# Two context pairs of the first batch: halves split in natural layout and turned by DMA transposes

## The chip, the core and the metric

The kernel runs on one core of one Trainium2 chip. The metric is the time of one execution of the program on the device, in microseconds (us): the median of several executions. The core has five engines, each with its own in-order stream of instructions: PE (TensorE: matmuls, and transposes as matmuls with an identity), DVE (VectorE), ACT (ScalarE), POOL (GpSimd) and SP (SyncE, which here issues every DMA). PEld is PE's loading of weights, which the profile shows apart.

## What is computed

A decoder layer with three sublayers, each followed by a residual sum and a layer norm, on x of 4 x 256 x 512 and a context of 4 x 1601 x 512, in fp32:

```python
x = _layernorm(x + attn(x, ...))           # attention over 16 features of a token, cheap
x = _layernorm(x + xattn(x, ctx, ...))     # nearly all of the work
x = _layernorm(x + ffn(x, ...))            # 64 experts' biases, top 8, cheap

# xattn: 32 query heads, 8 key/value heads of 128
kv = concatenate([context, latents], axis=1)          # 1857 tokens of each batch
q, k, v = latents @ Wq, kv @ Wk, kv @ Wv              # then by heads
q, k = rms_norm(q, q_norm_w), rms_norm(k, k_norm_w)
probs = softmax(q k^T / sqrt(128))
out = (probs v) @ Wo
```

## The kernel before

**Halves.** PE multiplies in fp16. To keep fp32's precision each operand is held as a high half (the value rounded to fp16) and a low half (what the rounding left), and each product is three matmuls: high by high, high by low, low by high (`mm3`, L237 to L243). A `split` (L88) makes the halves: ACT writes the high one (L90), then DVE, or POOL where it is told so, subtracts (L92; L94 where a scale is applied).

**Tiles and units.** The 1857 tokens of a batch are 15 tiles of up to 128 tokens, taken in eight pairs: pairs 0 to 5 are context, pair 6 is the two tiles of the latents (the 256 tokens of x after the first sublayer), pair 7 is the last, short tile of the context. A unit is one key/value head of one batch: 8 heads x 4 batches = 32 units, four query heads each. Per unit, each pair is projected (`kv_proj`, L390: the tile kvp in PSUM), its keys are normalized and split (`kv_n`, L416: the tile kh) and turned by a DMA transpose into KT (`kv_tr`, L431). Per query head come the scores s (`qk`), their copy S and maximum M, the exponentials P with their halves (L545 to L555) and the products o with the values (L574 to L576).

**Turning the input.** PE needs a pair's tokens with the features on the partitions. `kv_make` (L334) does that once per batch and pair, and leaves the halves in kvm, which is stored to DRAM (kvd, `kv_keep`, L364) and loaded again for later units. It has two ways. For the first batch: load the fp32 rows (cst, `src_load`), turn each of the two tiles with four PE transposes into the PSUM tile kvtp (L348), and split from there, ACT and DVE, 128x512 each. For the other batches: split the rows as they are, 128x1024 at once, into the tile nat (which has a single buffer), and turn both halves of both tiles with one DMA transpose (L359). The first batch's pairs stay in SBUF for the first two units, which are projected together. kvm has three buffers, the PSUM tiles six in turn, and kh shares a pool of five buffers with others.

**Order.** The order of the start-up is written out by hand in the string `START` (L29): its words name steps such as load4, make4 (kv_make of pair 4), proj4 (kv_proj for both first units), norm4, turn4, keep4. Between them stand the first sublayer (a0, a1: its results y are the latents), the weights' splits, the q projections. Everything after it is sorted by positions (`at`, L714) from the tables of numbers AT, F0 and LAST. A scheduler then orders the instructions of each engine by its own estimate of their times, so a change in one place can shift neighbours on every engine. An instruction waits at the head of its engine's stream until what it needs is there, and what stands behind it waits too.

Names that the steps use: st_q, st_kv and st_o are loaded weights of Wq, Wk/Wv and Wo before their splits into wq, wkv and wo; kss and krk are the sum of squares and the scale of k (POOL, L405 and L406); bnrs is the scale of a layer norm (POOL, L164); qn, qh and QT are q normalized, split and turned.

Of the kernel before, what the change touches and what calls it, by code (L numbers as in the profile page):

```python
# [19 lines left out]
XS = 1.0  # L20
# [22 lines left out]
          lexp=0.335, lexps=0.178, lpv=2.055, levac=1.151, lout=3.348, lqk=1.003, lqkw=0.833)  # L43

LAST = dict(maxb=0.352, exp=0.478, exps=0.207, evac=1.181, wout=3.893, qk=-2.845, qmax=1.507, norm=1.251, turn=2.762, wo=2.134, bkv=9.818, bq=5.434, bo=2.349, lq1=2.628, srcl=0.453, mke=-2.061, mktl=-1.69, s3i=-0.687, s3w=4.208)
F0 = dict(xm=1, maxt=0.133, maxb=0.145, exp=0.367, exps=0.122, pv=2.25, evac=0.972, out=3.422, wout=4.882, qk=-1.157,
          qmax=0.828, norm=0.349, turn=1.009, lead=3.36, wkv=8.299, wq=6.751, wqs=0.602, wq1=5.352, wo0=2.125,
          wo=0.038, lq1=2.522, l1lo=0.774, l1w=-1.506, srcl=0.65, mklo=0.296, mke=-2.739, mktl=-2.607, prep3=3.901,
          s3=5.222, s3i=0.334, s3w=5.192)
# [2 lines left out]
def tile_decoder(ctx: ExitStack, tc: tile.TileContext, x, cx, Wq1, bq1, Wk1, bk1, Wv1, bv1,  # L52
# [15 lines left out]
    TL = NF // 2  # L68
# [16 lines left out]
    def tps(name):  # L85
        return psu.tile([P, 512], F32, tag="u", name=name)

    def split(dst_h, dst_l, src, scale, eng=None):  # L88

        nc.scalar.activation(dst_h, src, AF.Copy, scale=scale)  # L90
        if scale == 1.0:
            (eng or nc.vector).tensor_tensor(dst_l, src, dst_h, ALU.subtract)  # L92
        else:
            nc.vector.scalar_tensor_tensor(dst_l, src, scale, dst_h, ALU.mult, ALU.subtract)  # L94
# [25 lines left out]
    def eng(k):  # L120
        return nc.gpsimd if k else nc.vector
# [186 lines left out]
    def nk(t):  # L308
        return REM if t == NT - 1 else P

    def kview(tile_, t):

        o = (t % 2) * 2 * NC * P
        return tile_[:, o:o + 2 * NC * P].rearrange("p (l c k) -> p l c k", l=2, c=NC)[:, :, :, :nk(t)]

    def tiles_of(p):
        return [t for t in (2 * p, 2 * p + 1) if t < NT]
# [16 lines left out]
    def kv_make(b, p):  # L334

        kt = pkv.tile([P, 2 * RW], F16, tag="kv", name=f"kvm_{b}_{p}")
        assert p != TL or {("x1", b, 0), ("x1", b, 1)} <= done
        if b == 0:
            for u in range(HB):
                kvt[u, p] = kt  # L340
            if p == NPAIR - 1:
                nc.gpsimd.memset(kt[:, :RW].rearrange("p (a k) -> p a k", k=P)[:, :, REM:], 0.0)
            for t in tiles_of(p):
                k = nk(t)
                tp = tps(f"kvtp_{b}_{t}")
                for c in range(NC):
                    sc = y[b, t - NF][:, c * P:(c + 1) * P] if p == TL else src[b, p][:k, t % 2, c * P:(c + 1) * P]
                    nc.tensor.transpose(tp[:, c * k:(c + 1) * k], sc, ident[:k, :k])  # L348
                v = kview(kt, t)
                split(v[:, 0], v[:, 1], tp[:, :NC * k].rearrange("p (c k) -> p c k", c=NC), XS)  # L350
        else:
            nat = p1.tile([P, 2, 2, E], F16, tag="nat", name=f"nat_{b}_{p}")
            n, k = len(tiles_of(p)), nk(2 * p)
            if k < P:
                nc.gpsimd.memset(nat[64:, 0], 0.0)
            for e, j in enumerate(range(n) if p == TL else (slice(0, n),)):
                sc = y[b, j] if p == TL else src[b, p][:k, j]
                split(nat[:k, j, 0], nat[:k, j, 1], sc, XS, eng(p == TL))
            nc.sync.dma_start(out=kt[:, :n * RW].rearrange("p (a k) -> p a k", k=P),  # L359
                              in_=nat[:, :n].rearrange("p j l e -> p (j l e)"), transpose=True)  # L360
        if b > 0:
            kv_keep(b, p, kt)

    def kv_keep(b, p, kt):  # L364
        nc.sync.dma_start(out=kvd[b][p][:, :width(p)], in_=kt[:, :width(p)])
        done.add(("kvd", b, p))
# [334 lines left out]
    for p in range(NPAIR):  # L701
        for k, f in (("load", src_load), ("make", kv_make), ("keep", lambda b, p: kv_keep(b, p, kvt[b, p]))):
            first[f"{k}{p}"] = lambda f=f, p=p: f(0, p)
        for k, f in (("proj", kv_proj), ("norm", kv_n), ("turn", kv_tr)):
            first[f"{k}{p}"] = lambda f=f, p=p: [f(u, p) for u in range(HB)]
# [15 lines left out]
    def par(u):  # L721
        return dict(AT, **F0) if u < KVH else dict(AT, **LAST) if u >= U - 4 else AT

# [6 lines left out]
    for b in range(1, B):  # L730
        A = par(KVH * (b - 1))
        t0 = 4 * (KVH * b - 1)
        lo = max(t0 + A["l1b"], A["l1lo"])
        for i in range(NQ):
            w = (t0 + A["l1w"] - lo) / NQ
            spread(lo + w * i, lo + w * (i + 1), stage1(b, i), 10)
        new = [p for p in range(NPAIR) if p != TL]
        lo = max(t0 + A["mkb"], A["mklo"])
        for k, p in enumerate(new):
            pos = lo + (t0 + A["mke"] - lo) * k / len(new)  # L740
            at(pos - A["srcl"], src_load, b, p)
            at(pos, kv_make, b, p)
        at(t0 + A["mktl"], kv_make, b, TL)
    for u in range(1, U):
        h, b = units[u]
# [14 lines left out]
    for u in range(U):  # L760
        h, b = units[u]
# [81 lines left out]
```

## Time and profile before

| | |
|---|---|
| runs of the kernel before | 2420.73 us median of 3 (2419.91 to 2424.31) |
| profiled execution | 2421.83 us, its span 2420.10 us |
| busy share of the span | PE 97%, PEld 83%, DVE 79%, ACT 85%, POOL 64% |
| granted TensorE clock, mean | 0.991 |
| DMA | 338.82 MB, 140 GB/s on average |
| `kv_make`, first batch | PE transposes L348 of cst x52; DVE splits of kvtp 128x512 x14, 677 ns each; ACT 604 ns each |
| `kv_make`, other batches | ACT splits of cst 128x1024, 1057 ns (median); DMA transposes L359 x24 |
| POOL subtraction L555, 128x1024 | 2148 ns each, x384 |

The span runs from the first to the last instruction; the time of an execution has a little around it. The profile gives each engine's busy time, and for each idle stretch of an engine the instruction or transfer that ended it ("<-"). The chain of waits follows the end back through what released what. Times in the lines are us from the start of the span: first the start, then the length. Ends of pipelined matmuls are modelled, so the pace of matmuls is read from their starts.

### The profile page before, as it was taken

Reading aid. Unit: us, or ns where it says so; the run is one execution under the profiler, and the core shown is the slowest. Engines: PE = TensorE matmul, PEld = TensorE weight load, DVE = VectorE, ACT = ScalarE, POOL = GpSimd, SP = SyncE. Lnnn points to the kernel's source line nnn. Section 1 sums busy time; section 2 is a strip of 40 time slices with the busy share of each in tenths; the row PEclk is TensorE's granted clock in tenths of the full one; section 3 lists DMA queues with packets and bytes.
Section 4 is the critical chain, followed back from the end, with each engine's and each line's share of the span. In section 5 each row is a group of like instructions: output and inputs, shape, how many; then the busy total and the mean of one; then the engine's idle time right before and its main releaser. Section 6 shows DMA issues by size and latency. Waiting matters only on the chain.

```text
span 2420.1 us, 65667 instructions
## 1 busy us (share of the span) xinstructions
PE 2347.3 (97%) x25424; PEld 2003.1 (83%) x25424; DVE 1909.9 (79%) x3747; ACT 2051.1 (85%) x4672; POOL 1538.5 (64%) x1367
## 2 busy tenths in 40 slices
PE   7799999999999999999999999999999999999997
PEld 5587888888888878888888888888888888888885
DVE  8788978987877788787777788787777778777775
ACT  4798898888888878889888888888889888889884
POOL 2377776776666655776656666666666655657554
PEclk9999999999999999999999999999999999999997
DMA  8946776666564546555545555455644543554310
GB/s 267 245 100 160 185 175 178 185 153 156 137 164 112 148 139 166 139 142 125 151 128 129 156 142 137 140 138 121 156 116 113 131 122 109 140 131 105 98 35 27
DMA packets 393345, 338.82 MB, mean 140 GB/s; under 512 B 318532, under 2 KB 328260, under 8 KB 384840
## 3 DMA queue, kind: packets, MB, share of 16 engines
q1 hardware_dynamic: 393032, 334.63, 53.0%
q8 instruction: 199, 3.26, 0.6%
q14 instruction: 114, 0.93, 0.2%
HBM read 219.98 MB, written 38.80 MB: 107 GB/s over the span
## 4 chain that ended last, share of the span: by engine, by line
PE 74%; ACT 8%; DVE 7%; issue 5%; POOL 4%; DMA 2%; SPq 0%; POOLq 0%; DVEq 0%; ACTq 0%
PE o L574 7%; PE o L576 7%; PE o L575 7%; PE kvp L241 7%; PE kvp L243 7%; PE s L241 7%; PE kvp L242 7%; PE s L243 7%; PE s L242 7%; PE wo L241 2%; PE wo L242 2%; PE wo L243 2%; POOL P L555 2%; DVE S L545 2%; ACT P L553 2%
## 5 line engine op out<-in xcount | busy, mean ns | idle before, releaser
L555 POOL TENSOR_TENSOR P<-S,P 128x1024 f16<-128x1024 f32 (+1 forms) x512 | 1032.3, 2027 | 435.3 <-ACT S L554 410.3
L574 PE MATMUL o<-Vh,P 128*128 128x129 f16 (+1 forms) x3840 | 696.1, 221 | 6.8 <-ACT P L553 2.9
L576 PE MATMUL o<-Vh,P 128*128 128x129 f16 (+1 forms) x3840 | 695.8, 220 | 3.6 <-POOL P L555 3.6
L575 PE MATMUL o<-Vl,P 128*128 128x128 f16 (+1 forms) x3840 | 695.0, 219 | 0.0
L498 ACT COPY S<-s 128x512 f32<-128x512 f32 (+1 forms) x1024 | 568.3, 594 | 81.8 <-PE s L243 75.4
L553 ACT ACTIVATE P<-S,lnps 128x1024 f16<-128x1024 f32 (+1 forms) x480 | 530.9, 1117 | 48.1 <-DVE S L545 46.8
L545 DVE TENSOR_TENSOR S<-S,mt 128x1024 f32<-128x1024 f32 (+1 forms) x512 | 557.8, 1146 | 13.1 <-PE mt L536 12.2
L554 ACT ACTIVATE S<-S,lnps 128x1024 f32<-128x1024 f32 (+1 forms) x480 | 538.4, 1126 | 0.2
L241 PE MATMUL s<-QT,KT 128*128 128x256 f16 x1920 | 524.0, 273 | 14.1 <-ACT S L498 3.1
L243 PE MATMUL s<-QT,KT 128*128 128x256 f16 x1920 | 523.9, 273 | 0.0
L242 PE MATMUL s<-QT,KT 128*128 128x256 f16 x1920 | 523.7, 273 | 0.0
L504 DVE TENSOR_TENSOR M<-s,M 128x512 f32<-128x512 f32 x640 | 438.5, 685 | 99.8 <-ACT S L498 79.6
L574 PEld LDWEIGHTS <-P 128*128 128x128 f16 (+1 forms) x3840 | 376.1, 98 | 24.6 <-DVE oh L593 3.3
L241 PE MATMUL kvp<-wkv_back,kv 128*128 128x256 f16 (+1 forms) x1440 | 392.6, 273 | 1.8 <-DVE rl L584 0.6
L243 PE MATMUL kvp<-wkv_back,kv 128*128 128x256 f16 (+1 forms) x1440 | 392.6, 273 | 0.0
L242 PE MATMUL kvp<-wkv_back,kv 128*128 128x256 f16 (+1 forms) x1440 | 392.6, 273 | 0.0
L575 PEld LDWEIGHTS <-P 128*128 128x128 f16 (+1 forms) x3840 | 377.4, 98 | 14.7
L576 PEld LDWEIGHTS <-P 128*128 128x128 f16 (+1 forms) x3840 | 375.6, 98 | 5.0 <-POOL P L555 3.8
L241 PEld LDWEIGHTS <-kv 128*128 128x128 f16 (+1 forms) x2040 | 201.5, 99 | 48.0 <-issue 8.0
L243 PEld LDWEIGHTS <-kv 128*128 128x128 f16 (+1 forms) x2040 | 201.4, 99 | 47.1
L242 PEld LDWEIGHTS <-kv 128*128 128x128 f16 (+1 forms) x2040 | 201.4, 99 | 41.4 <-issue 1.7
L241 PEld LDWEIGHTS <-KT 128*128 128x128 f16 x1920 | 188.0, 98 | 33.1 <-issue 5.5
(177 smaller groups left out, 4164.2 us busy)
## 6 DMA issues: line engine op xcount, KB each, us to landing
kv<-kvd SPq DMA_DIRECT2D x210, 512.0 KB, 3.7
wq_back<-wqd SPq DMA_DIRECT2D x24, 1024.0 KB, 6.2
wo_back<-wod SPq DMA_DIRECT2D x24, 1024.0 KB, 5.2
kvd<-kvm SPq DMA_DIRECT2D x28, 512.0 KB, 3.1
cst<-in_ctx_dram SPq DMA_DIRECT2D x24, 512.0 KB, 5.8
wkv_back<-wkvd SPq DMA_DIRECT2D x24, 512.0 KB, 4.2
st_q<-in_L_xattn_Wq_dram SPq DMA_DIRECT2D x17, 512.0 KB, 4.8
wqd<-wq SPq DMA_DIRECT2D x8, 1024.0 KB, 6.1
```

The costliest lines, as they stand in the source:

```text
L241: nc.tensor.matmul(dst, ah, bh, start=start and k == 0, stop=False, skip_group_check=skip)
L242: nc.tensor.matmul(dst, ah, bl, start=False, stop=False, skip_group_check=skip)
L243: nc.tensor.matmul(dst, al, bh, start=False, stop=stop and k == n - 1, skip_group_check=skip)
L498: nc.scalar.copy(sv, ps[:, :m, :])
L504: nc.vector.tensor_tensor(Mx[n], ps, Mx[n], ALU.max)
L545: nc.vector.tensor_tensor(sv, sv, Mb[n].unsqueeze(1).broadcast_to([P, m, S]), ALU.subtract)
L553: nc.scalar.activation(pt[:, 0, :m, :], sv, AF.Exp, bias=lnps, scale=ES)
L554: nc.scalar.activation(sv, sv, AF.Exp, bias=lnps, scale=ES)
L555: nc.gpsimd.tensor_tensor(pt[:, 1, :m, :], sv, pt[:, 0, :m, :], ALU.subtract)
L574: nc.tensor.matmul(a[:, :P + 1], ph, v1[:k], start=t == 0 and i == 0, stop=False, skip_group_check=True)
L575: nc.tensor.matmul(a[:, :P], ph, v0[:k], start=False, stop=False, skip_group_check=True)
L576: nc.tensor.matmul(a[:, :P + 1], pl, v1[:k], start=False, stop=t == NT - 1 and i == NQ - 1, skip_group_check=True)
```

## The change

For the first batch, pairs 4 and 5 take the way of the other batches: split as rows into nat and turned by one DMA transpose each. A bit mask, dm=48 (bits 4 and 5), picks them. In this way the first batch has its low halves subtracted on POOL; the other batches keep DVE, except for the latents' pair, which had POOL and keeps it. The store to kvd stays a step of its own for the first batch (keep4, keep5).

```diff
-F0 = dict(xm=1, maxt=0.133, ...
+F0 = dict(dm=48, xm=1, maxt=0.133, ...
...
         if b == 0:
             for u in range(HB):
                 kvt[u, p] = kt
+        turned = b > 0 or F0["dm"] >> p & 1
+        if not turned:
             if p == NPAIR - 1:
                 nc.gpsimd.memset(kt[:, :RW].rearrange("p (a k) -> p a k", k=P)[:, :, REM:], 0.0)
             for t in tiles_of(p):
...
         else:
             nat = p1.tile([P, 2, 2, E], F16, tag="nat", name=f"nat_{b}_{p}")
...
             for e, j in enumerate(range(n) if p == TL else (slice(0, n),)):
                 sc = y[b, j] if p == TL else src[b, p][:k, j]
-                split(nat[:k, j, 0], nat[:k, j, 1], sc, XS, eng(p == TL))
+                split(nat[:k, j, 0], nat[:k, j, 1], sc, XS, eng(b == 0 or p == TL))
             nc.sync.dma_start(out=kt[:, :n * RW].rearrange("p (a k) -> p a k", k=P),
                               in_=nat[:, :n].rearrange("p j l e -> p (j l e)"), transpose=True)
```

In the program's order this removes 16 PE transposes, four ACT and four DVE splits of 128x512, and adds two ACT splits and two POOL subtractions of 128x1024 and two DMA transposes on SP. The stores of pairs 4 and 5 now wait for a transpose's landing where they waited for DVE. The order of neighbouring instructions changes on every engine up to about 150 us of the profile before; after that it is the same.

More of the change, by code (lines that the diff above doesn't have):

```diff
@@ L45 @@
 LAST = dict(maxb=0.352, exp=0.478, exps=0.207, evac=1.181, wout=3.893, qk=-2.845, qmax=1.507, norm=1.251, turn=2.762, wo=2.134, bkv=9.818, bq=5.434, bo=2.349, lq1=2.628, srcl=0.453, mke=-2.061, mktl=-1.69, s3i=-0.687, s3w=4.208)
-F0 = dict(xm=1, maxt=0.133, maxb=0.145, exp=0.367, exps=0.122, pv=2.25, evac=0.972, out=3.422, wout=4.882, qk=-1.157,
+F0 = dict(dm=48, xm=1, maxt=0.133, maxb=0.145, exp=0.367, exps=0.122, pv=2.25, evac=0.972, out=3.422, wout=4.882, qk=-1.157,
           qmax=0.828, norm=0.349, turn=1.009, lead=3.36, wkv=8.299, wq=6.751, wqs=0.602, wq1=5.352, wo0=2.125,
```

## The prediction

> **What bounds the kernel now.** First I read the busy tenths in 40 slices, where PE (TensorE) is full from the third slice to the last but one; then the windows of the first 130 us, where the change lies (columns: sum, PE, PEld, DVE, ACT and POOL busy, granted clock, DMA share, GB/s).
>
> ```profile
> PE   7799999999999999999999999999999999999997
> ```
>
> ```profile
> 30.00:40.00 10.00, 7.18 (x59) 5.62 (x57) 10.00 (x23) 5.44 (x20) 6.34 (x7) 0.99 1.26 342
> 40.00:50.00 10.00, 10.00 (x80) 8.48 (x78) 10.00 (x19) 4.84 (x19) 2.23 (x4) 0.84 0.82 260
> 50.00:60.00 10.00, 9.35 (x87) 8.10 (x85) 10.00 (x23) 6.07 (x27) 4.23 (x8) 1.00 0.39 100
> 60.00:70.00 10.00, 9.34 (x75) 7.34 (x74) 6.59 (x20) 6.35 (x26) 4.59 (x12) 1.00 1.05 225
> ...
> 110.00:120.00 10.00, 2.21 (x21) 1.87 (x22) 9.17 (x12) 9.95 (x12) 6.84 (x4) 0.74 0.73 252
> 120.00:130.00 10.00, 10.00 (x124) 9.49 (x123) 7.19 (x11) 9.94 (x16) 9.90 (x6) 0.92 0.18 54
> ```
>
> From 30 to 60 us DVE is full and PE nearly so; POOL and DMA have room. From 120 us on PE is the bound. So the start-up is a chain that ends when PE begins its steady work at 118.48 us, and whatever moves that moment moves the end by as much. The chain of waits (start, length, what) names its links:
>
> ```profile
> 55.74 0.61 DVE kvm L92
> 56.40 0.28 PE kvp L243
> ...
> 82.16 6.63 DMA st_o<-in_L_xattn_Wo_dram
> ...
> 116.28 2.15 POOL P L555
> 118.48 0.29 PE o L576
> ```
>
> The reader should see a part led by DVE's splits and PE (to 66), a part that waits for the first Wo load (82 to 89), and the first softmax.
>
> **What goes.** Per changed pair, 8 transposes, 2 ACT and 2 DVE splits of 128x512. In the timeline PE is held about 0.44 us for each four transposes (48.42 to 48.86), DVE 0.60 us per split. Together PE loses 4 x 0.44 = 1.8 us of work and DVE 4 x 0.60 = 2.4. ACT has 4 x 0.60 against 2 x 1.06 now: nothing.
>
> **What comes.** Per pair one ACT split (1.06, the nat rows of the second batch), one POOL subtraction of 128x1024 and one DMA transpose of 128 x 16 x 128. POOL: L555 has the same tile size, 2.15 us; L224 on POOL took 3.40. I take 2.15 and keep 3.4 as the upper end. The transpose: 24 of the same line for the other batches.
>
> ```profile
> L359 SPq DMA_TRANSPOSE kvm<-nat x24: 1232/1986/6025, 101.3 to 1727.0; - x24
> ...
> DMA to landing us min/median/max: 3.0/5.3/8.9
> ```
>
> The last issue on SP before the first new one would be this:
>
> ```profile
> 45.12 2.09 SPq L437 DMA_TRANSPOSE KT<-kh  x1
> ```
>
> I take the median, 5.3 from issue to landing (3.0 and 8.9 are the ends; those within the first 400 us took 5.2 to 7.9): KT transposes between 48 and 61 us landed after 2.4 to 2.9, about their median of 2.5, so that stretch is calm. [...]
>
> **Step 1, pairs 4 and 5, path to 64.5 us.** The context tile of pair 4 is issued at 38.16 and lands 5.1 us later, at 43.3; ACT 44.3, POOL 46.5. SP is behind the KT issue above until 47.2, so the transpose lands at 52.5. PE ends pair 3 at 48.42 + 24 x 0.109 = 51.0, waits 1.5, and ends pair 4 (48 matmuls, 5.2) at 57.7; before it was 58.6. So pair 4 is covered. Pair 5 is not: nat has one buffer, so ACT's split of pair 5 waits for pair 4's transpose: ACT 52.5 to 53.6, POOL 55.7. SP, held until 52.5 because the store of pair 4 stands before the next KT transposes and waits for the landing, has issued the store and two KT (1.2 each) by 55.3. The transpose goes out at 55.8, lands at 61.1, and PE ends pair 5 at 66.3 instead of 64.5. **+1.8**; in general two landings L in series, 2 x (L - 5.3) more or less.
> Queued behind the waiting ACT split are pair 3's squares (53.6 instead of 50.65), behind POOL's subtraction pair 3's k scales and the layer-norm scale (about 59 instead of 55.5), behind SP's store the KT of pair 2 (52.9 instead of 48.95). DVE so applies the layer norm to x rows 0 at 59 instead of 57, rows 1 at 63.7 instead of 62.7: still before the transposes of the latents, which stand on PE after pair 5. Without that cover it would cost 1 us at most. KT of pair 2 gives a kh buffer back at 55.3; pair 4 wants it after 60.
>
> **Step 2, PE's clock.** PE would stand still from 58.1 to 61.1. These rows show what follows a gap of 2.15 us:
>
> ```profile
> 38.89 0.28 PE L243 MATMUL kvp<-wkv,kvm 128*128 128x256 f16 x1 [2.15 <-DVE kvm L92]
> ...
> 40.22 0.42 PE L241 MATMUL kvp<-wkv,kvm 128*128 128x256 f16 x1
> ```
>
> From 39.66 to 42.99 matmuls started every 0.213 us instead of 0.109: some 16 of them, 1.6 us lost. Gaps of 1.0 and 1.1 us (before 85.25 and 71.44) were followed by no such rows. For a gap of 3.0 I take **+1.2**, between 0 and 1.6, as it may begin late. [...]
>
> **Step 3, 66 to 118 us.** The order of the built program differs there too, until about 150 us; later it is the same on every engine. One part helps: the splits of the next wq come earlier on ACT, so that wkv_2, and after it the issue of the Wo load, come some 0.5 earlier (**-0.5**). One part hurts. ACT now has the first half of Wo ahead of the first four score copies, and the second half ahead of the wq_2 splits and the squares of the second head's q; DVE has them in the same places. Before, first DVE, then ACT:
>
> ```profile
> 87.13 1.12 DVE L459 SCALAR_TENSOR_TENSOR qn<-qp,qrq,wb 128x128 f32<-128x128 f32 x4 [1.48 <-POOL qrq L452]
> ```
>
> ```profile
> 88.82 1.06 ACT L90 ACTIVATE wo<-st_o 128x1024 f16<-128x1024 f32 x1 [1.23 <-DMA st_o<-in_L_xattn_Wo_dram]
> ```
>
> In before's clock: the load lands at 82.16 + 6.63 = 88.8, ACT 89.9, DVE 91.0, and only then q of the second head (92.1 instead of 88.2) and the first maxima. The second half's load is issued at 91.16 when DVE has read the first, lands 3.7 later at 94.9; ACT 95.9, then two wq_2 splits (2.0), then the squares at 97.9 instead of 93.15. DVE: second half of Wo to 97.2, wq_2 to 99.5, a maximum, q at 100.2 instead of 95.98, 4.2 late. Of the 12.4 us that DVE then took until the first subtraction of the softmax (108.36), 1.1 (Wo) is done already and 0.9 was idle, while one reduction (0.6) moves ahead: 111.2. **+2.8**. If both loads landed after 3.7, the second wait would be nearly gone and this term about +0.8.
>
> **Sum.** +1.8 + 1.2 - 0.5 + 2.8 = +5.3. The profiled execution took 2421.83 us, 1.73 more than its span of 2420.10; so 2427.1 for it. It lies 1.1 above the median of the runs shown, 2420.73, hence **2426.0** for the median. About 0.2%, 4.8 us, is what a measurement can tell here; the forecast lies just beyond it, at 0.22%.
>
> **Rivals.**
> A, *only the first wait* (0.22): Wo arrives in time, since its wait depends on what else is in the queue: 6.6 for one half, 3.7 for the other. Then 2420.7 + 1.8 + 1.2 - 0.5 + 0.8 = 2424.0.
> B, *the cover holds; not slower* (0.16): one mechanism, the two transposes in series. Pair 5 ends at 55.7 + 2L, so below L = 4.4 PE is no later than before, there is no gap and no slow clock, and the relief of DVE and PE (1.8 of the 2.4) can count: 2420.7 - 1.8 = 2418.9 with Wo in time; with both reliefs in full and the 0.5 of step 3, 2420.7 - 4.7 = 2416.0. [...] Against: the median, the 5.2 above, and that the 3.0 may belong to the half-size tile of the last pair, which this line issues too.
> C, *a crowded queue* (0.15): both land like the one at 101 us, after 7.9 (SP held 5.9): 5.2 more, 2431.2.
> That the change does nothing is excluded by the program's order: 16 transposes of PE are gone and two L359 transposes stand on SP between the KT issues.
>
> **How the numbers follow.** The forecast has 0.47: +3.2 to +8 us, of which 0.35 is beyond +4.8, as more of its open terms add than take away. Slower: 0.35 + 0.15 (C) = 0.50. Same: 0.12 of the forecast, 0.22 of A, 0.09 of B = 0.43. Faster by over 0.2%: 0.07, the lower part of B. Range: 2418.5 (B with Wo in time) to 2432.0 (C); POOL's 3.4 twice, +2.5 on the forecast, is inside. Left out are the lower part of B and the upper of C.
>
> **What the profile after would show.** Step 1: the two L359 issues near 47 and 56, ACT's nat split of pair 5 ended by the DMA kvm<-nat, PE idle before pair 5 ended by the same DMA, pair 5 ending near 66 to 68. Step 2: rows of 0.42 after that gap. Step 3: an ACT wait for st_o longer than 1.23 us, a second one at the other half, the first L545 near 114 to 116. The last sign: PE's first steady matmul near 124 instead of 118.48. It is wrong if transposes land under 4.4, if Wo lands before ACT asks for it, or if PE's steady stretch takes back what the start lost: it was full in 130 to 150, so I count on none.

## The result and the profile after

The changed kernel takes **2432.45 us** (median of 4, 2429.56 to 2435.22) against 2420.93 (median of 4) before: ratio 1.0043, 95% interval 1.0031 to 1.0055. It is slower by 11.5 us, more than twice the 5.3 forecast. The median lies 0.45 above the upper end of the forecast's range (2432.0), which is less than the interval can tell: by the ratio the time is 2431.3, between 2428.4 and 2434.2. Its profiled execution took 2431.76 us with a span of 2429.7 and a mean granted clock of 0.990; beside before's 2421.83 that is +9.9, and the readings below account for this 9.9. In the changed kernel every line number from L343 on is two higher.

The busy tenths of the changed kernel are still full from the third slice to the last but one. The windows (columns as before) show where the first 130 us differ:

```profile
PE   6799999999999999999999999999999999999996
```

```profile
30.00:40.00 10.00, 7.16 (x58) 5.63 (x57) 10.00 (x22) 4.78 (x16) 5.77 (x6) 0.98 1.18 322
40.00:50.00 10.00, 10.00 (x79) 8.19 (x78) 10.00 (x16) 5.64 (x19) 3.93 (x5) 0.85 0.99 251
50.00:60.00 10.00, 7.33 (x69) 6.25 (x67) 8.75 (x22) 5.65 (x26) 6.57 (x10) 1.00 0.78 200
60.00:70.00 10.00, 9.33 (x69) 7.64 (x67) 5.93 (x18) 5.54 (x23) 3.61 (x9) 0.83 0.93 172
...
110.00:120.00 10.00, 4.56 (x39) 3.05 (x37) 9.06 (x16) 5.12 (x7) 1.14 (x2) 0.90 1.10 249
120.00:130.00 10.00, 6.21 (x67) 5.88 (x66) 9.47 (x9) 9.97 (x14) 10.00 (x6) 0.58 0.46 158
```

From 50 to 60 us PE is busy 7.33 us instead of 9.35, and the granted clock from 60 to 70 is 0.83 instead of 1.00. From 120 to 130 PE is busy 6.21 us instead of 10.00: the steady part begins later. The transposes are 26 now, with SP held a little longer at the median (2.24 us against 1.99) and landing a little sooner (5.0 against 5.3):

```profile
L361 SPq DMA_TRANSPOSE kvm<-nat x26: 1232/2242/5726, 45.9 to 1737.4; - x26
...
DMA to landing us min/median/max: 3.0/5.0/9.3
```

PE's timeline shows where pair 5 starts and where the steady part starts:

```profile
59.00 0.28 PE L241 MATMUL kvp<-wkv,kvm 128*128 128x256 f16 x1 [2.31 <-DMA kvm<-nat]
...
60.15 0.42 PE L242 MATMUL kvp<-wkv,kvm 128*128 128x256 f16 x1
...
124.19 0.29 PE L578 MATMUL o<-Vh,P 128*128 128x129 f16 x1 [3.79 <-POOL P L557]
```

PE waits 2.31 us for pair 5's transpose, then runs at half speed (starts 0.21 us apart) from 60.0 to 63.4. The first steady matmul comes at 124.19 instead of 118.48, **+5.71**. A mark that every unit has, the moment at which DVE first reads its Wo product (y<-wo), is 5.76 us late at 215 us, 6.81 at 291, 9.14 at 364 and 9.8 at the last unit, at 2397. So the loss has two parts: 5.7 us in the start-up, and some 3.4 more between 215 and 364.

### The profile page after: what moved, and what is told of

Read it like the earlier page. It is cut to its first block, busy times and chain, and to the rows that moved or that the text cites. A ratio compares the mean times of both kernels' runs of the same rounds, so it can differ in the third digit from the quotient of the medians.

```text
span 2429.7 us, 65645 instructions
## 1 busy us (share of the span) xinstructions
PE 2348.5 (97%) x25408; PEld 2002.7 (82%) x25408; DVE 1912.0 (79%) x3743; ACT 2054.4 (85%) x4670; POOL 1544.8 (64%) x1369
## 4 chain that ended last, share of the span: by engine, by line
PE 53%; ACT 4%; DVE 3%; issue 1%; POOL 1%; DMA 1%; POOLq 0%; DVEq 0%; ACTq 0%
PE o L576 5%; PE o L578 5%; PE o L577 5%; PE s L241 5%; PE s L243 5%; PE s L242 5%; PE kvp L241 5%; PE kvp L242 5%; PE kvp L243 5%; PE wo L241 1%; PE wo L242 1%; PE wo L243 1%; DVE S L547 1%; ACT P L555 1%; PE qp L241 1%
```

## The experiments

All runs in one table. "Pair 5" is the start of the latents' transposes, which follow pair 5 on PE; "steady" is the first steady matmul; the three lags are those of the Wo mark behind before's at 215, 364 and 2397 us. Marks and lags are read from one execution of each kernel; up to about 43 us these executions already differ by as much as 1 us. The last columns compare medians with runs of before on the same chip.

| kernel | pair 5 | steady | lags | median, us | ratio (95%) |
|---|---|---|---|---|---|
| before | 64.52 | 118.48 | 0 | | |
| after | 65.92 | 124.19 | 5.8 / 9.1 / 9.8 | +11.5 | 1.0043 (1.0031 to 1.0055) |
| e1, pair 4 only | 65.32 | 124.53 | 6.6 / 8.1 / 8.1 | +10.2 | 1.0040 (1.0027 to 1.0052) |
| e3, low halves on DVE | 65.97 | 124.32 | 5.9 / 8.8 / 9.8 | +8.9 | 1.0027 (1.0015 to 1.0038) |
| e5, q ahead of pair 7 | 66.14 | 127.48 | 8.2 / 9.3 / 14.5 | +11.9 | 1.0052 (1.0039 to 1.0065) |
| e7, pair 5 delayed on PE | 65.60 | 123.99 | 6.1 / 6.4 / 8.1 | +7.7 | 1.0033 (1.0021 to 1.0046) |
| e11, after in before's order | 65.25 | 120.38 | 0.8 / 3.7 / 3.9 | +5.2 | 1.0020 (1.0011 to 1.0029) |
| e12, before in after's order | 64.22 | 123.75 | 4.8 / 4.3 / 5.0 | +3.9 | 1.0016 (1.0007 to 1.0024) |
| e13, of that the first part | 64.19 | 120.35 | 1.2 / 1.4 / 1.0 | +2.9 | 1.0008 (0.9999 to 1.0017) |
| e14, of that the second part | 65.39 | 123.35 | 4.4 / 4.7 / 1.1 | +1.5 | 1.0002 (0.9993 to 1.0011) |
| e15, two small loads | 64.14 | 117.60 | -2.0 / -1.9 / -3.8 | -1.1 | 0.9994 (0.9985 to 1.0003) |
| e16, own tile for pair 5 | 66.18 | 119.99 | 1.3 / 2.4 / 3.7 | +5.1 | 1.0022 (1.0013 to 1.0031) |
| e17, pair 4, before's order | 66.12 | 120.32 | 0.7 / 3.1 / 3.8 | +3.5 | 1.0013 (1.0004 to 1.0021) |
| e18, two idle transposes | 63.87 | 118.45 | 0.0 / -0.3 / -1.2 | -1.2 | 0.9995 (0.9986 to 1.0005) |

### First round: which part of the change costs

**e1**, only pair 4 turned, so nothing queues for nat twice:

```diff
-F0 = dict(dm=48, xm=1, ...
+F0 = dict(dm=16, xm=1, ...
```

> Only pair 4 takes the new way (dm=16); pair 5 is turned by PE. Theory (two landings in series through the one nat tile make pair 5 late, and the late pair 5 does the rest): pair 4's transpose lands while PE is still at pair 3, nothing waits, PE has lost 8 transposes (0.9 us), so the first steady matmul is at 117.5 to 119.5 and the time is that of the kernel before, -2 to +2 us. Rival (a DMA transpose and POOL's 2.1 us in the crowded start cost by themselves, about half of the whole change per pair): +4 to +7 us. Rival 2 (the 4 us lost between 220 and 440 us belong to any change of the order in the start): first steady matmul early or equal, and still +3 to +5 us at the end.

Measured +10.2. One pair costs nearly as much as two, so the serial landings are not the main price. The order that the scheduler wrote for this kernel has the same exchanges after 66 us as the order of after.

**e3**, the low halves on DVE instead of POOL:

```diff
-split(nat[:k, j, 0], nat[:k, j, 1], sc, XS, eng(b == 0 or p == TL))
+split(nat[:k, j, 0], nat[:k, j, 1], sc, XS, eng(p == TL))
```

> As the changed kernel, but the low halves of pairs 4 and 5 on DVE instead of POOL. Theory (the series of two landings counts): DVE needs about 1.2 us per subtraction where POOL needs 2.1, so both landings come earlier by 1 to 2 us in all, PE's wait before pair 5 falls from 2.3 to under 1.5 us, and the order written after it changes back only in part: -3 to +1 us against the changed kernel, that is +8 to +12 against the kernel before. Rival (DVE, full from 30 to 60 us, is what bounds the start, and POOL was the gain of the change): 2.4 us of subtractions come back to DVE, pair 5 later than 66 us, +12 to +15 against the kernel before.

Measured +8.9; the marks are those of after within 0.4 us, and the interval overlaps. POOL's part is at most a few us of the whole, and pair 5 is no earlier without it (65.97 against 65.92).

**e5**, an attempt to write the old q order into the hand-made string:

```diff
-    proj7 qnorm0 qproj1 norm7 keep6 turn3 keep2 qturn0 turn5 qnorm1 proj6 ...
+    qnorm0 qturn0 proj7 qproj1 norm7 keep6 turn3 keep2 turn5 qnorm1 proj6 ...
```

> The changed kernel with the first head's q steps (normalize, split, turn) named earlier in START, so that the program puts the wq_1 splits behind qh_0_0 again and the Wo splits behind the first score copies and the wq_2 splits. Theory (late pair 5 +2, the new order of wq_1 +1.9, of Wo +2.5): pair 5 ends near 66 as in the changed kernel, but the first subtraction of the softmax comes 2.5 to 4.5 us earlier than its 114.1, the steady matmuls at 120 to 122; if the 4 us lost between 220 and 440 us go with that order or with the late start, +2 to +5 us against the kernel before, if they are independent of it, +6 to +8. Rival (the order has no price, the waits only moved): the time of the changed kernel, +10 to +12 against the kernel before.

Measured +11.9, no better than after: the splits of the next wq came at 83.99 instead of after's 75.64, and the issue of the Wo load at 90.42 instead of 85.43. The scheduler rearranged other things, so this run decides nothing about the order; it only shows that the string does not fix it.

**e7**, before with nothing turned, and pair 5 made a little longer on PE by repeating matmuls of one tile:

```diff
-            mm3(ps[:k, j, :], [...])
+            for _ in range(2 if u == 0 and p == 5 and j == 0 else 1):
+                mm3(ps[:k, j, :], [...])
```

> The kernel before, with nothing turned by DMA; the 24 matmuls of pair 5 for one unit are done twice (the same result again), 24 x 0.109 = 2.6 us of PE. The program's order then shows the same two exchanges as the changed kernel: wq_1 splits ahead of qh_0_0, Wo splits ahead of the score copies. Theory (it is the lateness of pair 5 with the order that the scheduler writes for it, not the transposes themselves): steady matmuls near 124, +6 to +7 us at 130 us; at the end +9 to +12 if the loss between 220 and 440 us follows the start, +6 to +7 if it doesn't. Rival (the transposes, POOL's subtractions and SP's waits have a price of their own): only the delay shows, +2.6 us, 2 to 4.

The edit added 24 PE instructions, of which 12 are matmuls (the others load weights), so the delay is some 1.3 us by estimate (12 x 0.109) and pair 5 ended 1.1 later. Yet the steady part came 5.5 later and the median +7.7. A small lateness of pair 5 is enough to bring the same exchanges and most of the loss, with no transpose, no split and no POOL subtraction involved. The suspect is now the order.

### Second round: the order by itself

In these kernels a list ORDER holds the instruction numbers of each engine from 66 to about 150 us, and each instruction is tied behind the one ahead of it by an edge that only orders (it makes no engine wait). Their line numbers are some 75 to 85 higher. e15 and e18 below carry the list of before's own order and cost nothing, so the list itself has no price that shows.

```diff
+ORDER = [...]
...
+    for line in ORDER:
+        for early, late in zip(line, line[1:]):
+            tc.add_manual_dep(names[f"I-{late}"], f"I-{early}", ... NoSync ...)
```

**e11**: after, with the list of before.

> The changed kernel, pairs 4 and 5 turned by DMA as in it, but from pair 5's end on (66 us) every engine is held to the order of the kernel before. Theory (the price is the order that the scheduler writes after pair 5, not the transposes): pair 5 ends near 66 as in the changed kernel, its lateness of 1.4 to 2 us is all that is left, so the first steady matmul is at 119.5 to 121 and the end at +1 to +3 us against the kernel before; +4 to +6 if the loss between 220 and 440 us is a matter of any late start. Rival (transposes, POOL and SP in the start are the price): +9 to +12, as the changed kernel.

**e12**: before, with the list of after.

> The kernel before, nothing turned by DMA in the first batch, but from pair 5's end on every engine is held to the order of the changed kernel. Theory (the order is the price): pair 5 ends at 64.5 as before, the first steady matmul comes at 122 to 124 instead of 118.5, and the end is +4 to +6 us, or +8 to +10 if the loss between 220 and 440 us goes with this order. Rival (the transposes are the price): -1 to +1 us.

**e13**: before, with after's order up to the first score copies and its own from there.

> The kernel before with only the first half of the exchange: up to the first scores (85 us) every engine stands in the changed kernel's order (kvp of pair 7 ahead of q's matmuls on PE, wq_1 splits ahead of qh_0_0 on ACT and DVE), after that in its own. Theory: wkv_2 and with it the issue of the first Wo load come about 1.9 us later (84.1 instead of 82.2), and the first steady matmul 1.5 to 2.5 us later; the end +1.5 to +2.5 us. Rival (this stretch is covered by the wait for Wo anyway, the load lands earlier when it is issued later): -0.5 to +1 us.

**e14**: before, with its own order up to there and after's from there.

> The kernel before with only the second half of the exchange: up to the first scores its own order, after that the changed kernel's (Wo splits ahead of the first score copies and of the wq_2 splits). Theory: Wo issue at 82.2 as before, ACT and DVE held by the wait for the load, first subtraction of the softmax 2 to 3 us later than 108.4, first steady matmul at 120.5 to 121.5, the end +2 to +3 us; with the loss between 220 and 440 us, if that goes with this part of the order, +6 to +7. Rival (Wo has to be split somewhere before the first maxima, so the place costs nothing): -0.5 to +1 us.

At the first steady matmul the order alone (e12) costs 5.3 us, the turned pairs alone (e11) 1.9, both together 5.7. They do not add up there: the late pair hides in a wait that the order brings (ACT waits 2.29 us for the first half of Wo in e12, 1.39 in after). Over the whole time they do, within the intervals: +3.9 and +5.2 make 9.1, against +11.5 (7.5 to 13.3 by the ratio's interval). At the first steady matmul the part at wq alone (e13) brings 1.9 and the part at Wo alone (e14) 4.9, where 2 to 3 were expected. Of these, 0.9 is not the order's: pair 5 was late by it, after 6.83 us at half speed from 37.7 on (before: 3.41). Neither shows a loss by its interval over the whole time. The lag of e14 shrinks from 4.7 at 364 us to 1.1 at the end; what gives it back was not traced.

How the first part works shows in ACT's timeline, first after, then before:

```profile
72.72 0.28 ACT L451 ACTIVATE qn<-qp 128x128 f32<-128x128 f32 x1 [1.33 <-PE qp L243]
...
75.64 2.00 ACT L90 ACTIVATE wq<-st_q 128x1024 f16<-128x1024 f32 x2 [1.37 <-PE qp L243]
...
77.80 0.61 ACT L468 CAST qh<-qn 128x512 f16<-128x512 f32 x1
```

```profile
74.04 0.61 ACT L466 CAST qh<-qn 128x512 f16<-128x512 f32 x1
74.56 2.00 ACT L90 ACTIVATE wq<-st_q 128x1024 f16<-128x1024 f32 x2
```

In after the splits of wq stand ahead of the cast of q. They wait 1.37 us for the last product of the old wq, since wq has one buffer, and the cast waits behind them: 77.80 instead of 74.04. On PE, matmuls of pair 7 now stand ahead of those of the q product and hold it longer. The second part shows in ACT's two waits for Wo in after:

```profile
91.03 1.06 ACT L90 ACTIVATE wo<-st_o 128x1024 f16<-128x1024 f32 x1 [1.39 <-DMA st_o<-in_L_xattn_Wo_dram]
...
96.89 1.06 ACT L90 ACTIVATE wo<-st_o 128x1024 f16<-128x1024 f32 x1 [1.85 <-DMA st_o<-in_L_xattn_Wo_dram]
```

Both halves wait for their load with the score copies or the next q behind them. In e14, where ACT comes to them earlier, the waits are 3.30 and 1.88.

### Third and fourth round: what the turned pairs cost in the old order

e11 is only 0.8 us late at 215 us and 3.7 at 364. Was that the number of DMAs, the transposes, nat's single buffer, or POOL?

**e15**: before in its own order, with two loads of 128x8 more on SP, into tiles t of their own:

```diff
+        if b == 0 and p in (4, 5):
+            nc.sync.dma_start(out=t, in_=x[0, 0:P, 0:8])
```

> The kernel before with two DMAs more on SP and nothing else: loads of 128 x 8 numbers that nobody reads, standing where the changed kernel has its two new transposes; every other instruction keeps its place. It asks about the 2.5 to 3 us that the changed kernel and its copy in the old order lose between 290 and 370 us, where all orders are the same: in all four kernels with pairs 4 and 5 turned by DMA, and in none of the four that turn nothing by DMA, SP's issue of one later transpose (near 1440 us) lasts 2.8 us instead of 1.9, so two more DMAs on SP seem to shift something that repeats. Theory (the count of DMAs ahead decides when SP is held later): the start as before, 118 to 119 us at the first steady matmul, that issue near 1440 us at 2.7 us or more, and +2 to +4 us at the end. Rival (the loss comes from the lateness of the start or from chance): the issue near 1440 us at 1.9, and -0.8 to +0.8 us.

**e16**: e11 with the halves of pair 5 in a tile of their own, in the buffer that wo takes later:

```diff
+            if b == 0 and p == 5:
+                nat = p1.tile([P, 2, G, E], F16, tag="wo", name="nat_0_5x")...
+            else:
+                nat = p1.tile([P, 2, 2, E], F16, tag="nat", name=f"nat_{b}_{p}")
```

> The changed kernel held to the old order from 66 us on, as in the experiment before, and pair 5's halves in a tile of their own (in Wo's place, which is not used yet), so that its split need not wait for pair 4's transpose. Theory (two landings in series through one tile make pair 5 late): ACT's split of pair 5 comes near 47 to 49 instead of 51.5, PE doesn't wait before pair 5, its clock isn't slowed, pair 5 ends at 63.5 to 64.7 instead of 65.6, the first steady matmul at 117.5 to 119; end 0 to +1.5 us against the kernel before if that lateness was the whole price of turning by DMA, +2.5 to +4 if the loss between 290 and 370 us is a price of its own. Rival (POOL or the queue is what makes pair 5 late): pair 5 at 65.5 or later, +4 to +6.

**e17**: e11 with `dm=16`.

> Only pair 4 turned by DMA, and from 66 us on the old order. Theory (one landing alone is covered by PE's work on pair 3): no wait of PE before pair 4 beyond 0.5 us, pair 5 ends no later than before (64.5, less 0.9 for the transposes that PE is spared, so 63.6 to 64.7), first steady matmul at 117.5 to 118.7, end -1 to +1 us; with a price of the later stretch for one more DMA on SP, +2 to +4. Rival (the transposes cost wherever they stand): half of the +5.2 that the two pairs cost in this order, +2 to +3, already in the start.

**e18**: before in its own order, with two DMA transposes of 128 x 16 x 128 into a tile that nobody reads, where after has its two:

```diff
+        if b == 0 and p in (4, 5):
+            nc.sync.dma_start(out=spare, in_=W1...[:, 0:16 * P], transpose=True)
```

> The kernel before with two more DMA transposes of 128 x 16 x 128 on SP, of the first sublayer's weights into a spare tile that nobody reads, at the places of the changed kernel's two; every other instruction keeps its place, and PE, ACT, DVE and POOL do exactly what they did before. It asks what the 2 to 3 us are that the versions with turned pairs lost after 290 us even in the old order, and that two small copies didn't cost. Theory (the number of DMA transposes ahead shifts when SP is held in the issue of a later one): the issue near 1435 us lasts 2.7 to 3.2 us as in the turned versions (1.9 in the others), the one near 1725 us 1.8 (3.0 to 3.4 in the others), the first steady matmul at 118 to 119.5, and the end +2 to +4 us. Rival (a price of turning data that something waits for, or of a late start): issues near 1435 and 1725 us as in the kernel before, end -1 to +1 us.

e15 and e18 cost nothing that shows. In e18 SP was held 3.07 and 1.78 us by the two issues, and the steady part began at 118.45. The two later issues that the expectations speak of stayed near before's 1.90 and 3.37 us (e15 1.82 and 3.13, e18 1.90 and 2.78), while every kernel with turned pairs has 2.7 to 3.2 and 1.7 to 1.9 there; so the theory that the count of DMAs shifts them fell. Neither two more DMAs (-1.1 us) nor two more transposes (-1.2 us) cost anything here by themselves; what is left is that somebody waits for them, and the splits that feed them.

e16 took away the wait for nat, and PE no longer waited for the DMA before pair 5. But the second transpose went out only at 52.07 (55.72 in e11): on SP it stands behind the store of pair 3 (51.57), and DVE's split of pair 3 ended at 51.54. The reason is on DVE, since the two POOL subtractions now came close together. POOL, DVE and PE of e16, in turn:

```profile
44.38 2.14 POOL L169 TENSOR_TENSOR nat<-cst,nat 128x1024 f16<-128x1024 f32 x1 [5.37 <-ACT nat L167]
...
46.88 2.13 POOL L169 TENSOR_TENSOR nat_5x<-cst,nat_5x 128x1024 f16<-128x1024 f32 x1
```

```profile
45.02 1.65 DVE L304 TENSOR_TENSOR big<-big 128x128 f32<-128x128 f32 x1
...
46.92 2.36 DVE L292 TENSOR_TENSOR big<-big 128x256 f32<-128x256 f32 x1
```

```profile
51.59 0.28 PE L320 MATMUL kvp<-wkv,kvm 128*128 128x256 f16 x1 [2.95 <-DVE kvm L169]
...
52.19 0.42 PE L319 MATMUL kvp<-wkv,kvm 128*128 128x256 f16 x1
```

The second DVE operation takes 2.36 us here and 0.41 in after; the first takes 0.28 in before. Both DVE operations end right after POOL's: 46.67 after 46.52, 49.28 after 49.01. **POOL's subtraction held DVE.** DVE, which leads this part of the start-up, was late with pair 3, PE waited 2.95 us for it, and the clock fell to half. So e16 shows a price for one cause by putting another in its place: it does not tell how dear nat's single buffer is alone. Its total, +5.1, is that of e11.

e17 shows that pair 4 alone, in the old order, has the later loss too (0.7 at 215 us, 3.1 at 364). Its pair 5 ended at 66.12, 1.6 late, although only pair 4 was turned. DVE was 0.95 late at 42 us already, before the first subtraction on POOL, and POOL's hold then lengthened one operation from 0.28 to 1.05; together they are about the whole.

Two kernels that would have told POOL's hold from the rest, the low halves on DVE in the old order, with nat and with a tile of its own, were not run. That stays open.

### The later loss

The trace of after accounts for the 3.4 us between 215 and 364. The first part is again a DVE operation held by POOL. DVE of before, then POOL and DVE of after:

```profile
283.42 0.42 DVE L227 TENSOR_TENSOR ot<-ot,mx 128x128 f32<-128x128 f32 x1
```

```profile
288.39 4.26 POOL L557 TENSOR_TENSOR P<-S,P 128x1024 f16<-128x1024 f32 x2
```

```profile
289.19 1.48 DVE L227 TENSOR_TENSOR ot<-ot,mx 128x128 f32<-128x128 f32 x1
```

POOL's pair of subtractions takes 4.26, so the first ends near 290.5, and DVE's operation ends at 290.67. In before the operation meets POOL's subtraction just before its end. Nothing in the instructions differs; only the moment at which DVE gets there does. The operation takes 0.90 us in e17, 0.82 in e11, 0.41 in e13 and 0.47 in e18. DVE is then late with a maximum that PE waits for ahead of Wo, in before, then in after:

```profile
287.05 0.39 PE L241 MATMUL wo<-wo,OT 128*128 128x512 f16 x1 [1.63 <-DVE M L504]
```

```profile
293.86 0.39 PE L241 MATMUL wo<-wo,OT 128*128 128x512 f16 x1 [2.67 <-DVE M L506]
```

That is +1.04 of the +1.05 gained between the marks at 215 and 291 us. The rest, 2.33 up to 364, starts with nat: ACT's next split waits 2.45 us for the transpose of the pair before it, instead of 1.44 (e11: 2.55), because SP is held 5.63 us at that issue instead of 4.58. ACT is late with a score copy, and PE waits 1.50 instead of 0.82, after which it runs at half speed from 339.94 to 343.35. This costs 0.68 plus about 1.7. PE of before, then of after:

```profile
330.76 0.27 PE L241 MATMUL s<-QT,KT 128*128 128x256 f16 x1 [0.82 <-ACT S L498]
```

```profile
338.63 0.27 PE L241 MATMUL s<-QT,KT 128*128 128x256 f16 x1 [1.50 <-ACT S L500]
...
339.99 0.42 PE L242 MATMUL s<-QT,KT 128*128 128x256 f16 x1
```

e11 has the same three steps (waits of 2.02 and 1.49, then half speed from 334.97 to 338.38), some 2.6 of its 2.9. Between the marks at 215 and 364 us every kernel with turned pairs loses 1.1 to 3.4 (after 3.4, e3 and e11 2.9, e17 2.4, e1 1.5, e16 and e5 1.1), and those without at most 0.3 (e7 and e14 0.3; e12 gains 0.5). But losses in the steady part are not theirs alone: between the marks at 364 and 510 us e7 loses 5.4 and e12 2.4, after 0.5, and the lag of e7 falls from 11.8 to 8.1 by the end. Why turned pairs in the start should bring DVE and SP to the worse moment 230 us later isn't settled: the order of instructions there is before's in after and in all the pinned kernels.

## Where the prediction held and where it failed, step by step

**Sign and size.** Slower was the likeliest of the three outcomes (0.50), and it is slower. The size was forecast as 5.3 us; it is 11.5, or 9.9 between the two profiled executions. The term that was mis-sized is the steady part, put at nothing, where the profile shows some 4 us.

**Step 1, right in its mechanism.** The two issues stand at 45.93 and 54.73 (forecast 47.2 and 55.8), ACT's second split waited for the first transpose, pair 4 was covered but for 0.36 us, and PE waited for pair 5. The landings were 5.1 us (45.93 to the start of pair 4 at 51.03) and 4.3 (54.73 to 59.00), not 5.3 twice. By the step's own rule, 2 x (L - 5.3) with their mean of 4.7, the +1.8 becomes +0.6.

**Step 2, right here, but the length of the wait alone did not decide.** +1.2 was forecast, and the half-speed stretch of 3.4 us cost about 1.7 by estimate (half of it). One of its two examples is misread: PE waits 1.03 us before 85.25, but before 71.44 it has no idle time at all. Steps 1 and 2 together are then 2.3, against a measured +1.4 for pair 5, or 2.1 when the 0.7 us are added by which this execution was ahead up to 43 us. Forecast was +3.0. But e11 waited 2.39 us at the same place and kept its clock; the last section has both waits side by side:

```profile
60.00 0.28 PE L318 MATMUL kvp<-wkv,kvm 128*128 128x256 f16 x1 [2.39 <-DMA kvm<-nat]
...
60.99 0.27 PE L318 MATMUL kvp<-wkv,kvm 128*128 128x256 f16 x1
```

**Step 3, the first half wrong in sign.** The wq splits standing earlier on ACT were taken to bring the Wo load 0.5 earlier. It was issued at 85.43 instead of 82.16, +3.3, of which pair 5's lateness explains 1.4 and this step the other 1.9 (in e12, where pair 5 was 0.3 early, the order alone made it 1.6 later). The forecast moved the splits up and did not ask what they themselves wait for: the single buffer of wq, which PE frees after the q product, itself moved back. **This is the step that failed in the start-up.**

**Step 3, the second half about right.** +2.8 was forecast. The first subtraction of the softmax is at 114.08 instead of 108.36: 5.72 late, of which 3.27 came in with the issue of Wo, so 2.45. Both waits were there.

**The sum, right by chance.** +5.3 was forecast for the first steady matmul, +5.71 measured, but step 1 was overrated and the -0.5 was +1.9. And the terms are not the change's own price: e12 and e11 show that the order alone gives 5.3 and the turned pairs alone 1.9. The prediction treated the new order as a consequence to be priced; that it is set off by a small lateness of pair 5 alone, with nothing turned (e7), it did not see.

**"Whatever moves that moment moves the end by as much" and "I count on none" failed.** The second was meant for what the steady part might take back. The steady part took another 4.0 us (9.8 at the last unit against 5.8 at 215 us), 3.4 of it by 364: DVE and POOL that meet at a worse moment (1.48 us instead of 0.42), a longer hold of SP (5.63 instead of 4.58), and one more slow stretch of the clock (3.41 us). This is the step that left the forecast at half of what was measured.

**What was not counted at all: POOL held DVE.** Moving the subtractions to POOL was priced as free for DVE. The runs say otherwise: 0.28 us became 1.43 in after and 0.41 became 2.36 in e16, and in e3, where DVE does the subtraction, the first of these operations takes 0.29. So DVE lost 1.15 us at the first of after's two subtractions, about half of the 2.4 that the prediction had relieved it of. That this made after slower in the start is not shown: pair 5 waited for its transpose there, and e3 was no earlier.

**The rivals.** A fell: Wo's second wait was there (1.85). B fell: it needed landings under 4.4, and they were 5.1 and 4.3. C's time, 2431.2, is the nearest to the result, but its cause is not there: no landing of the two took 7.9, and in e18 two more transposes in the queue cost nothing.

## What to carry to other kernels

Where a scheduler writes the order by its own estimate, try a small edit twice: as it comes, and with the order of the rest held fixed. Here a third of the loss was the order, and a mere delay on PE brought it too. Before a moved instruction is counted as "earlier", look for what it waits for itself (a single buffer above all), and before work is moved from DVE to POOL, look at what DVE does beside it (here one of its operations took 1.43 us instead of 0.28). A start-up that was later by x did not make the end later by x: e14's lag shrank from 4.4 to 1.1, after's grew from 5.8 to 9.8.

## What the runs showed of the hardware

**POOL's hold.** In the traces of before and after, these DVE operations that started inside a POOL subtraction of 128x1024 (2.13 us) ended a time after it that goes by their size: ot<-ot,mx of 128 columns 0.15 us (10 of them, 0.32 to 1.48 us long; alone 0.28), sc<-sc,mx of 256 columns 0.28 us (4 of them, 1.83 to 1.95; alone 0.42), xt<-xt,ot of 512 columns 0.55 us (4 of them, 2.07 to 2.51; alone 0.68). Not every operation was held: M<-s,M of 512 columns took 0.69 us (median) inside a subtraction and 0.68 alone. The records give the start and the end of an operation; what it does between them they do not show.

**The half-speed stretches of the clock.** In the traces of before and after the granted clock is either full or half, and every half-speed stretch starts a whole number of 3.41 us after the first one; up to 2385 us they last 3.41, 6.83 or 10.24 us. By estimate 3.41 us at half speed cost up to 1.7 us (half of it). Take windows of 3.41 us on this grid, from 25 to 2380 us of the two traces: 11 at full speed were followed by one at half speed, and PE was busy 1.49 us or less in each of them; 1,351 were followed by another at full speed, and PE was busy 1.46 us or more in each of those. In one pair of waits the longer one was not followed by half speed: here are after's windows around its wait of 2.31 us before pair 5, then e11's around its 2.39:

```profile
56.63:60.05 3.42, 1.11 (x12) 0.95 (x11) 2.96 (x8) 2.07 (x10) 2.42 (x6) 1.00 0.69 144
60.05:63.46 3.41, 3.41 (x18) 2.43 (x17) 2.62 (x10) 1.27 (x5) 1.21 (x2) 0.50 1.30 282
```

```profile
55.07:58.49 3.42, 2.54 (x26) 2.18 (x23) 2.69 (x7) 1.89 (x10) 3.09 (x7) 1.00 0.75 135
58.49:61.90 3.41, 1.90 (x18) 1.72 (x19) 2.69 (x9) 1.74 (x10) 2.23 (x5) 1.00 0.60 93
```

The first wait lies within one window, which leaves PE 1.11 us of work; the second is shared by two windows, with 2.54 and 1.90. The waits of 1.50 (after, near 338 us) and 1.49 us (e11) left 1.30 and 1.53 in their windows and were followed by a slow one; before's 0.82 left 2.08 and was not. Up to 130 us the clock lost (half of the half-speed time) 6.8 us in before, about 12 in after, 3.4 in e11, 10.2 in e12 and about 12 in e14: steps of this size come and go between versions.

**SP's hold at a transpose.** In after the 26 issues held SP 1.2 to 5.7 us each. In e18 the two added ones held it 3.07 and 1.78 us, and the steady part began at 118.45 us, as in before (118.48).
